# Cross-attention with layer norm on one core: projecting the first query group by column halves, and scoring its first two tiles eight heads at a time

## The chip, the core and the metric

The kernel runs on one of the cores of a Trainium2 chip. A core has five engines that run their own instruction streams in order: TensorE (PE: matrix products; its weight loads are shown apart as PEld), VectorE (DVE), ScalarE (ACT), GpSimd (POOL) and SyncE (SP), which here only issues transfers. An engine waits where an instruction needs the result of another engine or a transfer. SBUF is the working memory; PE writes to PSUM, which has eight banks of 128 x 512 fp32 numbers.

The metric is the device time of one execution in microseconds. Before the change the median of three runs is 506.8 us (506.09 to 507.09).

## What is computed

```
qs = q @ wq                     # q = x: 4 batches x 2048 rows x 512, fp32
ks_, vs = k @ wk, v @ wv        # k = v = ctx: 4 x 77 x 512
scores = einsum('bhqd,bhkd->bhqk', qs, ks_) / sqrt(32)      # 16 heads of 32
attn_w = softmax(where(mask, -inf, scores))
out = einsum('bhqk,bhkd->bhqd', attn_w, vs) @ wo + q
return layernorm(out) * gamma + beta
```

There are 8192 query rows in all, 77 keys to a batch, sixteen heads, and a mask of rows by keys. Everything is fp32. The kernel gets near fp32 accuracy from TensorE's faster float32r format: each operand is split into a high part and the rest, and a product is three matmuls (high x high, high x rest, rest x high).

## The kernel before, in words

Rows are taken in 64 tiles of 128, and the queries are projected in groups of 512 rows, four tiles to a group. The queries of a group are four blocks `m` of 128 columns, that is, of four heads; a block takes twelve matmuls (four contraction steps `c` of three products) into one PSUM bank and is then copied to SBUF (`q_visit`, `q_evac`).

For a tile the stages are these. `scores` (L308): 32 products of 32 contraction rows and 64 query rows, which PE runs side by side, for all sixteen heads, into four banks; bank `j` holds the heads `4g + j`. `maxima` (L357, DVE, one instruction to a head): adds the mask bias, takes the row maximum, and writes the biased scores to SBUF. `exps` (L375, ACT, one to a head): the exponential, with its row sum. `recip` (L383, DVE) and `normalise` (L387, POOL): division by the sum. `transp` (L405, DVE) and `regroup` (transfers issued by SP): weights with keys on the partitions. Then, on pairs of tiles, `av` (L452, PE: weights times values), its split by ACT and DVE, `o_proj` (L546, PE), the residual, the layer norm and the store.

Nothing reorders the program: an engine does its instructions in the order in which the Python code emits them, so a call's place in the code is its place in five queues. From tile 6 on, the order comes from the strings `PAIR` and `ORDER`. The first tiles are done by a prologue written out line by line (L683 to L755) and by a loop over `u = 0, 2, 4` (L769), which handles the tiles `u` and `u + 1`. The table `early` (L759) says which query blocks are projected in which step.

The prologue in order:
- Eight warm-up matmuls and eighteen short ones (L691 to L694).
- Loads: the first 256 rows of group 0's x (transposed, from the array `xT0`) and the four row blocks of wq (L702), the context and wk, the mask, then the second 256 rows of x (L711).
- Queries of the first 256 rows: for each `c` the splits of x and wq, then twelve matmuls of 256 columns, three products for each of the four `m` (L715 to L731). The four banks are copied out at L735.
- Keys: 48 matmuls of 312 columns (L739), with the splits of the context and of wk ahead of them (L732).
- Splits of the second 256 rows of x (L742), `deal_last` (three copies on ACT that lay the last batch's context beside the others), then `q_visit(0, 0)`: 24 matmuls of 256 columns, which give blocks 0 and 1 of the second 256 rows in one bank (L204).
- The loads of wv (from two queues, behind a `gate` on POOL), the copies of the keys (`keys_evac`: per call one block by ACT and one by DVE), and the loads of x for groups 1 and 2 (L751 to L755). Group 1's x goes into the buffer in which wq was staged.

Step `u = 0` of the loop then has: scores and maxima of tile 0, around the copy of `q_visit(0, 0)`; the casts of group 1's x on ACT and the exponentials of tile 0; `q_visit(0, 2)` (blocks 2 and 3 of the second 256 rows); the loads of wo; scores and maxima of tile 1; the differences of wv (`split_wv`); the exponentials of tile 1; and on PE group 1's blocks 0 and 1. Tiles 0 and 1 use rows 0 to 255 of group 0, tiles 2 and 3 the others.

A transfer is issued when its queue comes to it; SP's queue also waits where a buffer is still being read.

## Time and profile before

| | |
|---|---|
| median of three runs | 506.8 us |
| the profiled execution | 508.02 us, of which its span 506.2 us |
| granted TensorE clock | 0.997 of full speed |
| PE idle from 5.07 to 40.65 us | 0.00 us |
| PE idle from 40.65 to 53.45 us | 0.00 us |
| PE idle from 53.45 to 76.85 us | 1.48 us |

The span reaches from the first to the last instruction of the profiled execution; what is beyond it, 1.8 us, lies around it. In the page and the views, a line of a timeline gives start and length in us, engine, source line, operation, the tile written and the tiles read, their shapes, and in brackets the idle time ahead with what ended it. A line of the chain of waits gives start, length, engine, tile and line. A line of the stretches gives the busy time and count of PE, PEld, DVE, ACT and POOL, then the granted clock, the share of the transfer engines, and GB/s. Matmuls overlap, and the ends of their records are modelled.

### The profile page before, as it was taken

Reading aid. Unit: us, or ns where it says so; the run is one execution under the profiler, and the core shown is the slowest. Engines: PE = TensorE matmul, PEld = TensorE weight load, DVE = VectorE, ACT = ScalarE, POOL = GpSimd, SP = SyncE. Lnnn points to the kernel's source line nnn. Section 1 sums busy time; section 2 is a strip of 40 time slices with the busy share of each in tenths; the row PEclk is TensorE's granted clock in tenths of the full one; section 3 lists DMA queues with packets and bytes.
Section 4 is the critical chain, followed back from the end, with each engine's and each line's share of the span. In section 5 each row is a group of like instructions: output and inputs, shape, how many; then the busy total and the mean of one; then the engine's idle time right before and its main releaser. Section 6 shows DMA issues by size and latency. Waiting matters only on the chain.

```text
span 506.2 us, 20441 instructions
## 1 busy us (share of the span) xinstructions
PE 497.0 (98%) x6908; PEld 391.7 (77%) x6908; DVE 463.0 (91%) x2567; ACT 473.0 (93%) x2240; POOL 427.6 (84%) x384
## 2 busy tenths in 40 slices
PE   9999999999999999999999999999999999999995
PEld 7987678777777877777787777778777777777784
DVE  6698899999989988999998998999999889999997
ACT  6798899999999999999999999999999999999971
POOL 0559367989988988989998888999988888999995
PEclk9999999999999999999999999999999999999998
DMA  8945867677887778878777877877778787677665
GB/s 314 388 168 149 222 187 194 190 196 202 231 229 218 223 201 219 229 209 229 213 219 211 232 199 223 229 224 227 216 196 221 199 247 235 170 189 222 167 210 208
DMA packets 58280, 109.50 MB, mean 216 GB/s; under 512 B 9203, under 2 KB 10739, under 8 KB 58176
## 3 DMA queue, kind: packets, MB, share of 16 engines
q1 hardware_dynamic: 55776, 103.35, 71.7%
q0 software_dynamic: 1872, 4.20, 2.8%
q8 instruction: 55, 0.90, 0.8%
q10 hardware_dynamic: 528, 0.66, 0.4%
q14 instruction: 49, 0.40, 0.3%
HBM read 41.68 MB, written 16.78 MB: 115 GB/s over the span
## 4 chain that ended last, share of the span: by engine, by line
PE 79%; DVE 8%; ACT 7%; DMA 2%; issue 1%; SPq 1%; POOL 0%; POOLq 0%; DVEq 0%; ACTq 0%
PE pq L192 27%; PE po L564 26%; PE pa L459 10%; ACT pbuf L379 7%; PE sc L321 6%; DVE B L413 2%; PE sc L564 2%; DVE pbuf L364 2%; PE sc_e L321 2%; PE pk L218 1%; PE pq L725 1%; PE pq L190 1%; PE sc_f L321 1%; SPq L425 1%; DMA out<-o 1%
## 5 line engine op out<-in xcount | busy, mean ns | idle before, releaser
L379 ACT ACTIVATE pbuf<-pbuf,nm 128x77 f32<-128x77 f32 x1024 | 352.6, 349 | 8.6 <-DVE nm L364 7.8
L379 ACT ACTIVATION_READ_ACCUMULATOR pbuf<-pbuf,nm 128x1 f32 x1024 | 193.9, 189 | 0.0
L390 POOL TENSOR_TENSOR pbuf<-pbuf,ri 128x1232 f32<-128x1232 f32 x63 | 145.9, 2316 | 20.8 <-DVE ri L385 17.4
L364 DVE CUSTOM_DVE_ANT_0 pbuf<-sc,mb 128x77 f32<-128x77 f32 x828 | 143.9, 231 | 6.9 <-PE sc L321 6.4
L192 PE MATMUL pq<-xtl,wqh 128*128 128x512 f32 (+1 forms) x256 | 98.3, 384 | 0.0
L192 PE MATMUL pq<-xth,wql 128*128 128x512 f32 (+1 forms) x256 | 98.2, 384 | 0.0
L413 DVE STREAM_TRANSPOSE B<-pbuf 128x1280 f32<-128x1280 f32 x63 | 94.6, 1503 | 0.4
L564 PE MATMUL po<-woh,AH 128*128 128x512 f32 x224 | 90.7, 405 | 0.0
L192 PE MATMUL pq<-xth,wqh 128*128 128x512 f32 (+1 forms) x230 | 88.6, 385 | 0.0
L564 PE MATMUL po<-wol,AH 128*128 128x512 f32 x224 | 87.3, 390 | 0.0
L592 POOL TENSOR_TENSOR o<-o,gam 128x512 f32<-128x512 f32 x53 | 68.7, 1295 | 21.5 <-ACT o L588 21.5
L564 PE MATMUL po<-woh,AL 128*128 128x512 f32 x224 | 86.5, 391 | 0.0
L364 DVE DVE_READ_ACCUMULATOR2_ANT nm<- 128x1 f32 x1024 | 84.4, 82 | 0.0
L593 POOL TENSOR_TENSOR o<-o,bet 128x512 f32<-128x512 f32 x53 | 68.3, 1289 | 4.2
L180 POOL TENSOR_TENSOR xtl<-xtf,xth 128x1024 fp32r<-128x1024 f32 x28 | 67.4, 2409 | 0.1
L459 PE MATMUL pa<-PT,vsb 96*32 96x256 f32 x960 | 58.2, 382 | 1.6 <-DVE vsb L267 1.0
L321 PE MATMUL sc<-kct,q 32*64 32x77 f32 x3312 | 56.0, 238 | 0.5 <-DVE q L209 0.5
L192 PEld LDWEIGHTS pq<-xth,wql 128*128 128x128 f32 x256 | 48.2, 188 | 8.4
L192 PEld LDWEIGHTS pq<-xtl,wqh 128*128 128x128 f32 x256 | 48.1, 188 | 8.4
L321 PEld LDWEIGHTS sc<-kct,q 32*64 32x64 f32 x3312 | 49.3, 130 | 6.5 <-issue 4.4
L564 PEld LDWEIGHTS po<-woh,AH 128*128 128x128 f32 x224 | 42.0, 188 | 10.7 <-DVE nm L364 0.4
L192 PEld LDWEIGHTS pq<-xth,wqh 128*128 128x128 f32 x230 | 43.2, 188 | 9.0
(191 smaller groups left out, 855.1 us busy)
## 6 DMA issues: line engine op xcount, KB each, us to landing
PT<-B SPq DMA_DIRECT2D x355, 128.0 KB
xtf<-xT SPq DMA_DIRECT2D x28, 512.0 KB
o<-x SPq DMA_DIRECT2D x56, 256.0 KB
out<-o SPq DMA_DIRECT2D x56, 256.0 KB
PT<-B POOLq DMA_DIRECT2D x16, 128.0 KB, 4.5
o_end<-x SPq DMA_DIRECT2D x7, 256.0 KB
out<-o_end SPq DMA_DIRECT2D x7, 256.0 KB
xtf<-xT SPq DMA_DIRECT2D x4, 256.0 KB
```

The costliest lines, as they stand in the source:

```text
L180: nc.gpsimd.tensor_tensor(l, fx.pop((g, c)), h.bitcast(F32), ALU.subtract)
L190: nc.tensor.matmul(pq[:, cols], wc, r[:, c, cols], start=False, stop=False)
L192: nc.tensor.matmul(pq, wc, r[:, c, rs], start=(n == 0), stop=(n == 11))
L321: nc.tensor.matmul(scs[t][g, j][r0 : r0 + n], qd[t // 4][q, g, at : at + n], kct[q, g, t // TPB, keys_of(j)], start=True, stop=True,)
L364: nc.vector.tensor_tensor_reduce(pb[:, i // 2, (i % 2) * NK : (i % 2 + 1) * NK], scs[t][g, j], mb[:, t % TPB, keys_of(h)], -1.0, CEIL, ALU ...
L379: nc.scalar.activation(p, p, AF.Exp, bias=nmax[t][:, i : i + 1], scale=-1.0, accum_out=sums[t][:, i : i + 1])
L390: nc.gpsimd.tensor_tensor(pv, pv, rv.to_broadcast((P, NP, 2, NK)), ALU.mult)
L413: nc.vector.transpose(bt.rearrange("p c q r -> p q c r"), pbuf[t % NPB].rearrange("p q (c r) -> p q c r", c=5),)
L459: nc.tensor.matmul(pas[b, g // 2][HD * j : HD * (j + 1), (g % 2) * BLK : (g % 2 + 1) * BLK], vsb[:, 2 * b // TPB, HD * h : HD * (h + 1)], ...
L564: nc.tensor.matmul(pos[t], a[:, c, rs], w[:, c], start=(first and n == 0), stop=(n == 11))
L592: nc.gpsimd.tensor_tensor(o, o, gam, ALU.mult)
L593: nc.gpsimd.tensor_tensor(o, o, bet, ALU.add)
```

## The change

Group 0 is projected with all its 512 rows in each matmul, but in two column halves. The first half (blocks 0 and 1, heads 0 to 7) stands where the first 256 rows stood, ahead of the keys: 24 matmuls of 512 columns. So wq is now stored and loaded by column halves, the first half with x at the start and the second where the second 256 rows of x were loaded; x is loaded whole, one contraction step to a transfer. The second half of wq is split behind wk.

Behind the keys come at once the scores of heads 0 to 7 of tiles 0 and 1 (`scores_first((0, 1))`), with their maxima; then the other two query blocks, and then the scores of heads 8 to 15 of both tiles. Block 3 is copied out by ACT (rows 0 to 255) and DVE (rows 256 to 511), each half of the bank (`q_evac_both`). The exponentials of heads 0 to 7, the casts of group 1's x and ACT's half of that copy share ACT in a written-out order. `deal_last` moves between the two calls of `keys_evac`, the first two differences of wv go ahead of the copy of block 3 and the other two behind the second maxima, and the loads of wo, the identity and the first `recip` and `normalise` follow them. In step `u = 2` the first two differences of wo move on POOL from ahead of group 2's x differences to behind them. Step `u = 0` is no longer in the loop.

```diff
     def q_evac(g, m):
+        nc.vector.tensor_copy(qd[g][:, m, :], qp.pop((g, m)))
+
+    def q_evac_both(g, m):
         pq = qp.pop((g, m))
-        if g: ...
+        for cols, copy in zip(HALVES, (nc.scalar.copy, nc.vector.tensor_copy)):
+            copy(qd[g][:, m, cols], pq[:, cols])
...
+    def scores_first(gs):
+        own = [bank(f"sc_0_{gs[0]}_{j}") for j in range(GH)]
+        units = [(t, g) for g in gs for t in (0, 1)]
...
+        for t, g in units:
             for half in range(0, P, P // 2):
                 for j in range(GH):
                     score(t, g, j, half, P // 2)
...
-    for c in range(0, NC_D, 2):
-        nc.sync.dma_start(f0[c][:, 0], xT0[0, :, c : c + 2])
-        (nc.sync if c else nc.scalar).dma_start(stage_a[:, 0, c], wview(wq, c))
-        nc.sync.dma_start(stage_a[:, 0, c + 1], wview(wq, c + 1))
+    wqf = stage_a[:, 0].rearrange("p c e -> p (c e)").rearrange("p (a c e) -> p a c e", a=2, c=NC_D)
+    for c in range(NC_D):
+        nc.sync.dma_start(fx[0, c // 2 * 2][:, c % 2], xT[0, :, c])
+        if c < 2:
+            nc.scalar.dma_start(wqf[:, 0, c], wq[:, 0, c])
+        elif c == 2:
+            nc.sync.dma_start(wqf[:, 0, 2:], wq[:, 0, 2:])
...
     load_mask(0)
     for c in range(0, NC_D, 2):
-        nc.sync.dma_start(f0[c][:, 1], xT0[1, :, c : c + 2])
+        nc.sync.dma_start(wqf[:, 1, c : c + 2], wq[:, 1, c : c + 2])
...
-        for n, (w, r) in enumerate(((wqh, x0h), (wqh, x0l), (wql, x0h))):
-            for m in range(NG):
+        prods = ((wqh, x0h), (wqh, x0l), (wql, x0h)) if c else ((wqh, x0h), (wql, x0h), (wqh, x0l))
+        for n, (w, r) in enumerate(prods):
+            for m in range(2):
                 nc.tensor.matmul(
-                    pq0[m][:, :BLK],
+                    pq0[m],
...
+    for c in range(NC_D):
+        split_wq(1, c)
+    nc.scalar.copy(qd[0][:, 0], pq0[0])
+    nc.vector.tensor_copy(qd[0][:, 1], pq0[1])
...
-    deal_last()
-    q_visit(0, 0)
     mask_bias(0, slice(0, TPB // 2))
     gate(stage_a[:, 1, NC_D - 1, D - 1 :])
     load_wv()
-    for m in range(0, NG, 2):
-        keys_evac(pks, m)
+    keys_evac(pks, 0)
+    deal_last()
+    keys_evac(pks, 2)
...
+    heads_a, heads_b = ([GH * g + j for j in range(GH) for g in gs] for gs in ((0, 1), (2, 3)))
+    scores_first((0, 1))
+    maxima_of(0, heads_a)
+    maxima_of(1, heads_a)
+    q_visit(0, 2)
+    q_visit(0, 3)
+    q_evac(0, 2)
+    exps_of(0, heads_a[:3])
+    cast_xT(1, 0)
+    split_xT(1, 0)
+    exps_of(0, heads_a[3:7])
+    cast_xT(1, 2)
+    split_xT(1, 2)
+    exps_of(0, heads_a[7:])
+    exps_of(1, heads_a[:2])
+    mask_bias(0, slice(TPB // 2, TPB))
+    split_wv((0, 1))
+    q_evac_both(0, 3)
+    exps_of(1, heads_a[2:])
+    scores_first((2, 3))
+    maxima_of(0, heads_b)
+    maxima_of(1, heads_b)
+    exps_of(0, heads_b)
+    split_wv((2, 3))
+    load_wo()
...
+    recip(0)
+    normalise(0)
+    exps_of(1, heads_b)
+    evac = visits(1)
+    for q in evac:
+        q_visit(*q)
+    for u in range(2, JOIN, 2):
```

`maxima_of` and `exps_of` are `maxima` and `exps` with a list of heads; `split_wq(a, c)` makes the high part and the rest of half `a`, step `c`, of wq, the high parts on ACT but for the very first, which DVE makes.

## The prediction

> **What bounds the kernel now.** I began with the page's busy times, because they say which engine can't be made later without making the end later.

> ```profile
> span 506.2 us, 20441 instructions
> ...
> PE 497.0 (98%) x6908; PEld 391.7 (77%) x6908; DVE 463.0 (91%) x2567; ACT 473.0 (93%) x2240; POOL 427.6 (84%) x384
> ```

> PE is idle for only 506.2 - 497.0 = 9.2 us. The busy times by stretch say where; the columns are PE, PEld, DVE, ACT, POOL, then clock and DMA.

> ```profile
> 5.07:40.65 35.58, 35.58 (x396) 32.10 (x397) 29.22 (x136) 30.53 (x124) 17.98 (x15) 1.00 0.78 281
> ...
> 53.45:76.85 23.40, 21.92 (x355) 16.11 (x353) 20.81 (x119) 21.38 (x111) 10.92 (x9) 1.00 0.75 199
> 106.20:450.00 343.80, 343.72 (x4937) 269.06 (x4930) 321.38 (x1869) 338.41 (x1632) 312.31 (x259) 1.00 0.78 215
> ```

> From its first real matmul at 5.07 to 40.65 PE never stops. In the middle 344 us it stops for 0.08 us, and ACT is close behind (338.41 of 343.80). So whatever the start gains or loses on PE reaches the end unchanged, unless the ramp between 53.45 and 76.85, where PE idles 1.48 us, swallows or returns it. The third view is the chain of waits, where the change lies: start, length, what.

> ```profile
> 0.73 3.54 DMA xtf<-xT
> 4.29 0.72 ACT xth L154 x2
> 5.07 5.98 PE pq L725 x48
> 11.05 7.03 PE pk L218 x48
> 18.08 2.87 PE pq L192 x24
> 20.95 0.88 PE sc L321 x55
> 21.83 3.06 PE pq L192 x24
> 24.89 0.88 PE sc L321 x55
> 25.77 5.67 PE pq L192 x24
> 31.44 0.88 PE sc L321 x54
> 32.32 2.96 PE pv L258 x12
> 35.28 5.44 PE pq L192 x24
> 40.72 0.89 PE sc L321 x54
> 41.93 4.97 ACT pbuf L379 x29
> 47.73 1.45 DVE B L413
> ```

> It is PE's program order from 5.07 to 41.6: first half of group 0's queries, keys, second half in two visits with the scores of tiles 0 and 1 between them, group 1's queries, scores of tile 2, values, group 1 again, scores of tile 3. Only then do exponentials (ACT) and transposes (DVE) carry the chain. The two waits that matter to ACT are these.

> ```profile
> 33.27 1.98 ACT L176 CAST xth<-xtf 128x1024 fp32r<-128x1024 f32 x2
> ...
> 41.93 0.36 ACT L379 ACTIVATE pbuf<-pbuf,nm 128x77 f32<-128x77 f32 x1 [1.18 <-DVE nm L364]
> ```

> ACT is done with the exponentials of tiles 0 and 1 at 33.27, and later waits 1.18 us for tile 3's maxima, which wait for the scores that PE reaches at 40.65. ACT's earlier work is thus not on the path: only the moment at which PE reaches tile 3's scores counts. The question is how much the change moves that moment.

> **Part 1: fewer, wider query matmuls.** Before, group 0 takes 96 matmuls of 256 columns: 5.98 + 2.87 + 3.06 = 11.91 us of the chain. After, it takes 48 of 512 columns. A 512-wide run of 24 costs 5.44 behind other matmuls (35.28) and 5.67 behind a score visit (25.77). The first of the two runs begins the chain: a 256-wide run of 48 costs 2 x 2.87 = 5.74 in the stream and 5.98 at the start, so a start adds 0.24; 5.44 + 0.24 = 5.68. The second run comes behind scores: 5.67. Together 11.35, a gain of 0.56 us on PE.

> [...]

> **Part 2: the start.** Each of the four contraction steps still needs 384 KB (128 of x and 256 of wq before, 256 and 128 after), and the splits on ACT and DVE have the same total width.

> ```profile
> 4.32 0.69 PE L694 MATMUL pw<-ident 128*128 128x32 bf16 x18
> ...
> 5.02 0.62 ACT L154 CAST wqh<-stage_a 128x512 fp32r<-128x512 f32 x1
> ...
> 7.13 0.62 ACT L154 CAST wqh<-stage_a 128x512 fp32r<-128x512 f32 x1 [1.05 <-DMA stage_a<-wq]
> ```

> The warm-up matmuls end at 5.01, so PE can't begin earlier by more than 0.06. The first x cast is now 512 wide (0.62) and, from the same landing at 4.27, ends at 4.91: PE still begins at about 5.07. The third weight block landed at 7.13; PE needs its counterpart at 5.07 + 5.68 / 2 = 7.9, behind a 256-wide cast. I take 0 for the start, with bounds of -0.06 and +0.5 (two steps that wait 0.25 each, half of that DMA wait in all). The changed order of the first three products and ACT's second DMA issue are covered by the same wait for the first landing; uncovered, each would delay PE by its own length.

> **Part 3: from the keys to the first scores.** PE leaves the keys at 5.07 + 5.68 + 7.03 = 17.78 (18.08 before, so 0.30 earlier). Before, 2.87 us of queries covered the copying of the keys; now eight-head scores come directly behind them.

> ```profile
> 14.59 0.52 ACT L251 CAST ctx_h<-ctx_h 128x384 fp32r<-128x384 f32 x1
> 15.01 0.36 ACT L251 CAST ctx_lAH<-ctx_lAH 128x192 fp32r<-128x192 f32 x1
> 15.26 0.36 ACT L251 CAST ctx_lAL<-ctx_lAL 128x192 fp32r<-128x192 f32 x1
> 16.80 0.55 ACT L232 ACTIVATE kct<-pk 128x308 f32<-128x308 f32 x2 [1.18 <-PE pk L218]
> ...
> 17.24 0.62 DVE L234 TENSOR_SCALAR kct<-pk 128x308 f32<-128x308 f32 x2 [0.92 <-PE pk L218]
> ```

> The first visit needs only key blocks 0 and 1, whose copies end 0.30 earlier than these, at 17.05 (ACT) and 17.56 (DVE): before 17.78, so no wait. If this cover of 0.22 us fails, PE waits by the difference. ACT then deals the last batch's context columns (15.62 - 14.59 = 1.03) and copies block 2 (0.55), until 18.63, which nobody needs before the second visit. The scores take 0.88: the first visit ends at 18.66, 3.2 us earlier than tile 0's sixteen heads did (21.83); now it is eight heads of two tiles.

> **Part 4: the wait that is added.** Behind that visit PE runs 5.67 us of queries, to 24.33, and next come the second eight heads of both tiles. They need the fourth query block, whose last matmul has only just gone by. Before, each score visit used queries that had been copied out long ago. So PE stands still for one copy.

> ```profile
> L736 ACT COPY q<-pq x2: 362/368/374, 13.0 to 13.3; 128x256 f32<-128x256 f32 x2
> ...
> L737 DVE COPY q<-pq x2: 412/414/416, 13.9 to 14.2; 128x256 f32<-128x256 f32 x2
> ...
> 31.05 0.39 PE L192 MATMUL pq<-xth,wql 128*128 128x512 f32 x1
> 31.37 0.95 PE L321 MATMUL sc<-kct,q 32*64 32x77 f32 x64
> ```

> Tiles 0 and 1 read rows 0 to 255, the half that ACT copies in 0.37. A handoff costs about 0.06 (in the chain the x cast ends at 4.29 + 0.72 = 5.01 and PE starts at 5.07); I take one on each side, though no row shows them here. 24.33 is the last matmul's end, as 31.05 + 0.39 = 31.44 is in these rows. So the visit begins at 24.33 + 0.06 + 0.37 + 0.06 = 24.82 and, no longer overlapped with the matmul ahead (the row says 0.95 against 0.88), ends at 25.77. Before it ended at 25.77, too. The wait has eaten what the wider matmuls brought. Bounds of the wait: 0.36 (the copy alone) and 0.96 (both halves in turn, 0.37 + 0.41, with three handoffs). Queued behind PE's wait are all of group 1's queries.

> ACT must be free by 24.39. The exponentials run at this pace, and ahead of the copy stand ten of them and two casts.

> ```profile
> L379 ACT ACTIVATE pbuf<-pbuf,nm 128x77 f32<-128x77 f32 x32 | 11.0, 350 | 0.0
> ...
> 19.36 1.05 ACT L176 CAST xth<-stage_a 128x1024 fp32r<-128x1024 f32 x1 [1.12 <-DMA stage_a<-xT]
> 21.33 1.05 ACT L176 CAST xth<-stage_a 128x1024 fp32r<-128x1024 f32 x1 [0.93 <-DMA stage_a<-xT]
> 22.29 0.36 ACT L379 ACTIVATE pbuf<-pbuf,nm 128x77 f32<-128x77 f32 x1
> ```

> Thirty-two lie between 22.29 and 33.27: 0.343 each. The first can start some 0.3 behind the visit (41.93 against 40.72 + 0.89), at 19.0; a cast in a row of two takes 0.99 (33.27). Three end at 20.0; cast to 21.0; four to 22.4; cast to 23.4; three to 24.4: just in time. It needs the two x transfers at 20.0 and 22.4, against 19.36 and 21.33 in the trace: 0.6 and 1.1 us to spare. DVE has sixteen maxima, a copy, a mask piece and two of wv's differences before its half; PE does not wait for that half.

> **Part 5: what moves behind cover.** The second column half of wq is split where the second half of x was, in the same 2 us before the keys end. The halves of wv's differences move to both sides of the second visit; values need them at 32.32, some 3 us later. Uncovered, values would start late by what is missing there. wo's loads, the identity and wo's differences are not used before the transposes of tile 2 (47.73); the first two normalisations come earlier on POOL than before. Uncovered, they would push those transposes, one for one. ACT ends tiles 0 and 1 at 19.0 + 32 x 0.343 + 1.98 + 0.37 = 32.3 rather than 33.27, and then waits about 0.9 us longer for tile 3.

> **Sum.** -0.56 + 0.49 (the wait) + 0.07 (0.95 - 0.88) = **0.0 us** at 25.77, carried to the end. The profiled execution took 508.02 us for a span of 506.2; it would become 508.0 and 506.2. The unprofiled median, 506.8 of runs between 506.09 and 507.09, becomes **506.8**; about 0.2% (1.0 us) is what a measurement can tell from no change.

> **Rivals.** *Slower: the late x transfer.* The second piece of group 1's x goes into the buffer where the second half of wq now lies, so SP can issue it only when DVE has split that half: at about 15.3, when the next load went out that waited for such a split, and no longer by 13.12.

> ```profile
> 12.32 0.80 SPq L753 DMA_DIRECT2D stage_a<-xT  x2
> 15.27 0.93 SPq L171 DMA_DIRECT2D xtf<-xT  x2
> ```

> If it lands later by the same 2.5 us, at 23.8 instead of 21.33, the cast ends at 24.8, three exponentials at 25.8, the copy at 26.2, and the second visit begins at 26.3, 1.4 us later: 508.2. It decides from a landing after 22.4. For it: ACT is strictly in order and waited 0.93 for this transfer. Against: it took over 8 us from issue to landing, so it stood in a queue, and the queue's order is unchanged. *Waiting for both halves.* Both copies read one bank; if the scores wait for DVE's half too, 0.45 more: 507.2. *Faster: ACT's lead counts.* ACT is 98% busy in the middle stretch. If ACT is what the later stretches wait for, its lead of 33.27 - 32.3 = 0.9 us reaches the end: 505.9, and 505.8 with the wait's low bound. Against it stands the wait of 1.18 at 41.93, which would simply grow. [...]

> **How the numbers follow.** Forecast 0.59, both halves 0.10 (also within 0.2%), late transfer 0.13, ACT's lead 0.18. The lead lies on the bound of 0.2%; I count two thirds of it as faster. So faster is 0.12, no change 0.59 + 0.10 + 0.06 = 0.75, slower 0.13. The forecast's own range is 505.9 to 507.6: the bounds of start and wait (-0.2 and +0.5) and the runs' spread (-0.7 and +0.3). For the lead I reach down to 505.3, half the spread below its 505.8, and for both halves, with their spread, up to 507.9; what is left out is the late transfer and a little of the lead.

> **What would show it.** Right: 24 matmuls of 512 columns from 5.07, first exponential near 19.0, PE idle some 0.5 us before the second visit at about 24.8, tile 2's scores within 0.2 us of 31.4 and tile 3's of 40.7, and ACT's wait at 41.9 grown to about 2 us. Wrong: tile 3's scores moved by over 0.5 us, or the same start and yet another time at 76.85.

## The result, and the profile after

The kernel after the change took 511.27 us (median of 8 runs, 508.69 to 513.77) against 506.88 us before (8 runs, 506.09 to 508.78): a ratio of 1.0081, 95% interval 1.0053 to 1.0109. Measured again beside later experiments it took 509.49 us (12 runs, 508.57 to 514.02) against 506.90: 1.0063, interval 1.0041 to 1.0085. So the change makes the kernel slower by 2.6 to 4.4 us, where the forecast was no change.

The page of the profiled execution (512.25 us) begins:

```profile
span 510.1 us, 20346 instructions
...
PE 499.6 (98%) x6860; PEld 390.2 (76%) x6860; DVE 467.2 (92%) x2568; ACT 474.2 (93%) x2242; POOL 428.1 (84%) x384
```

There are 48 matmuls fewer, as planned, and yet PE is busy for 2.6 us longer. The chain of waits shows where the start goes (start, length, what):

```profile
0.73 3.57 DMA stage_a<-wq
...
4.32 6.99 DMA stage_a<-wk
...
11.32 0.63 ACT woh L153
...
11.98 0.70 DVE wol L154
...
12.73 7.03 PE pk L214 x46
19.76 0.88 PE sc L332 x52
20.64 5.67 PE pq L191 x24
26.31 0.45 PE sc L332 x32
...
26.77 0.53 PE sc L332 x32
27.30 5.67 PE pq L191 x24
...
42.25 0.88 PE sc L332 x52
...
55.38 1.86 PE pa L476 x32
```

Before, the start of the chain was PE's own work from 5.07 on. Now a transfer of wk carries it: it is issued at 4.32 and ends 7 us later, and only then can that part of wk be split. Two of the 48 key matmuls run ahead of it; the other 46, which the chain shows, run from 12.73 on, where before all 48 ran from 11.05 on. PE leaves the keys at 19.76 instead of 18.08, 1.68 us later, and tile 3's scores are 1.53 us late (42.25 against 40.72). The stretches show the transfers at that time; the last three columns are the clock, the share of the transfer engines and GB/s. First before, then after:

```profile
5.00:6.00 1.00, 0.94 (x9) 0.96 (x9) 1.00 (x3) 0.95 (x2) 0.00 (x0) 1.00 1.04 326
6.00:7.00 1.00, 1.00 (x11) 1.00 (x10) 1.00 (x3) 0.08 (x1) 0.00 (x0) 1.00 1.04 393
```

```profile
5.00:6.00 1.00, 1.00 (x4) 0.81 (x4) 0.68 (x2) 0.63 (x2) 0.00 (x0) 1.00 0.75 158
6.00:7.00 1.00, 1.00 (x6) 0.82 (x5) 0.97 (x2) 0.40 (x2) 0.00 (x0) 1.00 0.77 246
```

Where 326 and 393 GB/s were moved, there are now 158 and 246. In after's ACT timeline the splits wait for it, above all for wq's last piece:

```profile
5.37 0.62 ACT L153 CAST xth<-xtf 128x512 fp32r<-128x512 f32 x1 [0.58 <-DMA xtf<-xT]
...
6.89 0.62 ACT L153 CAST xth<-xtf 128x512 fp32r<-128x512 f32 x1 [0.60 <-DMA xtf<-xT]
...
8.70 0.40 ACT L724 CAST wqh<-stage_a 128x256 fp32r<-128x256 f32 x1 [1.18 <-DMA stage_a<-wq]
```

PE, which before never stopped here, stands still until that split is done:

```profile
9.15 0.73 PE L752 MATMUL pq<-xth,wqh 128*128 128x512 f32 x2 [0.76 <-ACT wqh L724]
```

The second loss is far away. PE's timeline near 429 us, with the idle time and its releaser in brackets: first one row of before (its second profile, `before2` below), where the 64 products of this visit run through in 0.95 us, then after, then after's stretches around it:

```profile
427.04 0.95 PE L321 MATMUL sc<-kct,q 32*64 32x77 f32 x64
```

```profile
428.68 0.94 PE L332 MATMUL sc<-kct,q 32*64 32x77 f32 x62
431.22 0.29 PE L332 MATMUL sc<-kct,q 32*64 32x77 f32 x2 [1.60 <-issue]
```

```profile
432.00:434.00 2.00, 2.00 (x7) 1.55 (x6) 2.00 (x11) 2.00 (x13) 1.95 (x3) 0.67 0.35 87
434.00:436.00 2.00, 2.00 (x6) 1.54 (x5) 2.00 (x19) 2.00 (x13) 2.00 (x3) 0.50 0.30 69
436.00:438.00 2.00, 2.00 (x10) 1.64 (x10) 1.97 (x5) 2.00 (x14) 1.85 (x2) 0.98 0.84 233
```

In the middle of a score visit, two products before its end, PE stands still for 1.60 us and waits for nothing that the profile shows. Then the granted clock falls to 0.67 and 0.50, which loses 0.66 + 1.00 us more. This is most of why PE's busy time grew: the same matmuls at a lower clock. The page of the profile names one more thing that could run dry there, TensorE's program itself, which arrives by a queue of its own:

```profile
q8 instruction: 54, 0.88, 0.8%
```

That is 0.88 MB in 54 packets, 16 KB each, for 2 x 6860 = 13,720 matmuls and weight loads: an estimate from these is 64 bytes to an instruction (0.88 MB / 13,720) and about 254 instructions to a packet (13,720 / 54), which the experiments below take as 256. In the stretch from 428 to 429 us the view of the transfers shows one of these packets (0.02 MB). That the queue is TensorE's shows in before and `g1_period` (fourth batch), which differ in the warm-up alone: the second has 256 instructions of TensorE more, and one packet more.

```profile
q8 instruction: 55, 0.90, 0.8%
```

```profile
q8 instruction: 56, 0.92, 0.9%
```

### The profile page after: what moved, and what is told of

Same layout as the page of the kernel before. It is cut to its first block, busy times and chain, and to the rows that moved or that the text cites. A ratio compares the mean times of both kernels' runs of the same rounds, so it can differ in the third digit from the quotient of the medians.

```text
span 510.1 us, 20346 instructions
## 1 busy us (share of the span) xinstructions
PE 499.6 (98%) x6860; PEld 390.2 (76%) x6860; DVE 467.2 (92%) x2568; ACT 474.2 (93%) x2242; POOL 428.1 (84%) x384
## 4 chain that ended last, share of the span: by engine, by line
PE 86%; ACT 4%; DVE 4%; DMA 3%; issue 1%; POOL 0%; SPq 0%; POOLq 0%; ACTq 0%
PE pq L191 30%; PE po L581 28%; PE pa L476 11%; PE sc L332 7%; ACT pbuf L396 3%; PE sc L581 2%; PE sc_e L332 2%; PE pv L254 2%; DMA PT<-B 1%; PE pk L214 1%; DMA stage_a<-wk 1%; PE pq L189 1%; PE sc_f L332 1%; DMA stage_a<-wq 1%; DVE pbuf L378 1%
## 5 line engine op out<-in xcount | busy, mean ns | idle before, releaser
L191 PE MATMUL pq<-xth,wql 128*128 128x512 f32 x248 | 97.6, 393 | 0.0
L191 PE MATMUL pq<-xtl,wqh 128*128 128x512 f32 x248 | 97.4, 393 | 0.0
L191 PE MATMUL pq<-xth,wqh 128*128 128x512 f32 x222 | 87.8, 396 | 0.0
L191 PEld LDWEIGHTS pq<-xtl,wqh 128*128 128x128 f32 x248 | 47.0, 189 | 8.9
L191 PEld LDWEIGHTS pq<-xth,wql 128*128 128x128 f32 x248 | 47.0, 189 | 8.9
L191 PEld LDWEIGHTS pq<-xth,wqh 128*128 128x128 f32 x222 | 42.1, 190 | 9.5
```

What stands on the lines that cost most here:

```text
L191: nc.tensor.matmul(pq, wc, r[:, c, rs], start=(n == 0), stop=(n == 11))
```

## The experiments

**First batch: start, place in the program, or chance.** `a1_pad` adds 48 warm-up matmuls (96 instructions with their weight loads), so that behind the warm-up TensorE's program stands where it stood in before.

```diff
-WARM = 8
+WARM = 3
-    for i in range(18):
+    for i in range(71):
```

> The changed kernel with 3 long and 71 short warm-up matmuls instead of 8 and 18: 48 more PE matmuls, so that from group 1 on PE's instructions stand at the same places of its 256-instruction blocks as in the kernel before; the short ones take about as long as the long ones left out, and PE waits for its loads there anyway. Theory A (PE's program is fetched in blocks, and a shift by 96 instructions puts a block's end ahead of dense score visits, where PE runs dry and the clock then drops): no stall of over 1 us in the middle, about 507.2 us (before plus the 0.4 us by which the ramp's end was late). Theory B (the late loads of the start are what is paid): no change, about 511. Theory C (such stalls come by chance in any program): a spread as wide as that of the changed kernel, about 511.

`b1_shift` does the reverse to the kernel before: 80 matmuls (160 instructions) more, which is 96 fewer modulo 256.

```diff
-WARM = 8
+WARM = 1
-    for i in range(18):
+    for i in range(105):
```

> The kernel before with 1 long and 105 short warm-up matmuls instead of 8 and 18: 160 PE instructions more, which is the changed kernel's shift of -96 but for one block of 256; nothing else changes. Theory A: a stall of 1 to 2 us in the middle in some or all runs, 508 to 511 us. Theory B: as before, 506.9 (plus up to 0.3 if the warm-up ends later). Theory C: as before, 506.9.

`a2_layout` is after with other host arrays: each piece of group 0's x and of wq is contiguous. In after the pieces are rows of 1 or 2 KB that lie 8 KB apart from partition to partition.

```diff
-        nc.sync.dma_start(fx[0, c // 2 * 2][:, c % 2], xT[0, :, c])
+        nc.sync.dma_start(fx[0, c // 2 * 2][:, c % 2], xT0[c])
...
-            nc.scalar.dma_start(wqf[:, 0, c], wq[:, 0, c])
+            nc.scalar.dma_start(wqf[:, 0, c], wqa[c])
...
-            nc.sync.dma_start(wqf[:, 0, 2:], wq[:, 0, 2:])
+            nc.sync.dma_start(wqf[:, 0, 2:], wqb[0])
```

> The changed kernel with group 0's x and wq stored so that each of the first transfers reads one contiguous piece of memory; the transfers and their order stay. If the 2 KB pieces that lie 8 KB apart are what slows the start: over 350 GB/s between 5 and 7 us (158 and 246 in the changed kernel), and the keys begin about 1.5 us earlier, near 11.2 us. Theory B: then about 507 us. Theory A: the stall stays somewhere in the middle, 509 to 511 us, since the ramp had already swallowed all but 0.4 us of the late start.

`a3_both` is `a2_layout` with the warm-up of `a1_pad`.

> Both: contiguous first transfers and 48 more warm-up matmuls. PE's first real matmul waits for the warm-up here if that takes longer than the loads. Theory A: no stall in the middle, 506.9 to 507.3 us. Theory B: 507 as well. Theory C: 509 or more with a wide spread.

Medians beside 506.89 for before: `a1_pad` 509.23 (1.0040, interval 1.0027 to 1.0053), `b1_shift` 509.03 (1.0041, 1.0029 to 1.0053), `a2_layout` 507.97 (1.0023, 1.0014 to 1.0032), `a3_both` 507.02 (1.0015, 0.9997 to 1.0033). The layout takes most of the loss back, and layout and warm-up together all that can be measured. With the layout mended the loads move 358 and 407 GB/s from 5 to 7 us and the keys begin at 11.50, about as expected if the scattered rows slow the start. Theory A had `a1_pad` at 507.2 and theory B at 511, and for `a2_layout` it was 509 to 511 against 507; both came out between the two. So neither the start nor the place in the program carries the loss alone. Most telling is PE's timeline of `b1_shift`, a kernel that has nothing of the change but a shifted program:

```profile
427.70 0.92 PE L321 MATMUL sc<-kct,q 32*64 32x77 f32 x61
429.15 0.35 PE L321 MATMUL sc<-kct,q 32*64 32x77 f32 x3 [0.52 <-issue]
```

It stops in the same visit as after. `a2_layout`, also shifted, has 0.69 us there, while `a1_pad` and `a3_both` have no such stop. `a1_pad` proves less than was hoped: its warm-up ended at 4.29, PE then stood still for 0.97 us, and up to 8.8 us its pairs of query matmuls took 1.03 us or more, where later pairs take 0.62. PE also had a gap of 0.89 us at 494 us. Slow first pairs show in `a2_layout` too (1.21 and 1.05 us, then 0.62), so what its start still loses need not come of the loads.

**Second batch: which array, which wait, which profile.** `c1_x` is after with x alone contiguous, `c2_wq` with wq's pieces alone.

> The kernel after, with group 0's x stored contiguously for each contraction step (in after each partition's 2 KB lie 8 KB apart); wq stays as in after. After's keys start at 12.73 us, with both x and wq contiguous at 11.50, before at 11.05. Theory X (the scattered x is what slows the loads): keys start near 11.5 and the loads move about 400 GB/s from 5 to 7 us. Theory Q (the scattered halves of wq, pieces of 1 and 2 KB, slow them): keys still start near 12.7, and the rate still falls below 250 GB/s between 5 and 7 us. Theory XQ (each carries part, by bytes in pieces of 2 KB): near 12.1.

> The kernel after, with the pieces of wq's column halves stored contiguously; x stays as in after. Theory X: keys still start near 12.7. Theory Q: near 11.5, at about 400 GB/s from 5 to 7 us. Theory XQ: near 12.1.

None of the three theories held. The chains, first of `c1_x`, then of `c2_wq`:

```profile
11.29 7.04 PE pk L215 x48
```

```profile
11.43 7.05 PE pk L215 x48
```

Either array alone brings the keys from 12.73 back to about 11.4, and between 5 and 7 us the loads move 386 and 380 GB/s (`c1_x`), 326 and 356 (`c2_wq`). So it is not one slow array: only x and wq together, both as rows 8 KB apart, bring the rate of these two microseconds down to 158 and 246. Scattered x alone costs less: in `c2_wq` PE waits 0.65 us for x's first cast and begins at 5.66. Why the two together lose so much stays open.

`c3_order` is after with the second visit of scores in the other order.

```diff
-        for t, g in units:
+        for t, g in units[2:] + units[:2] if gs[0] else units:
```

> The kernel after, with the second visit of scores in the other order: first the 32 products that read the query block 3, which has only just been copied, then the 32 that read block 2. In after the visit ends 0.99 us behind the last matmul ahead of it, 0.11 more than the 0.88 of a visit that waits for nothing, where the prediction had 1.44. Theory W: the copy does take the predicted 0.49 us, but the visit begins with 32 products that need block 2 only, and they fill the wait; then it is uncovered here, the visit ends about 1.4 us behind the matmul, and tile 2's scores come 0.4 later from the keys' start than in after (20.6 instead of 20.2 us). Rival: the wait itself is as short as 0.11 us; then the visit stays at 0.99.

PE's timeline of `c3_order`:

```profile
25.39 0.39 PE L191 MATMUL pq<-xth,wql 128*128 128x512 f32 x1
26.24 1.13 PE L332 MATMUL sc<-kct,q 32*64 32x77 f32 x64 [0.46 <-ACT q L207]
```

Now the wait stands open: 0.46 us, for ACT's copy, and the visit ends at 27.37, 1.59 us behind the last matmul (25.78) instead of 0.99. Theory W is right in kind: the wait was there and had been covered. The visit ends 0.2 us later than the expected 1.4, since its products take 1.13 us instead of 0.95, and why they do stays open.

`before2` is the kernel before, profiled once more.

> The kernel before, profiled a second time. Its first profiled execution took 508.02 us against a median of 506.88 and had a gap of 1.00 us on TensorE ahead of the first product of weights and values (53.84 to 54.84 us), which no profile of a changed kernel has. If that gap belongs to the one execution: no gap here, that product begins near 53.9 us, and the span is near 505.1. If it belongs to the kernel: the gap is here again, and the start's delay in after was partly swallowed by it.

Its chain, and the stretch of the ramp:

```profile
10.94 7.03 PE pk L218 x48
...
53.73 1.86 PE pa L459 x32
```

```profile
53.45:76.85 23.40, 22.89 (x446) 17.02 (x444) 21.68 (x124) 22.36 (x113) 12.15 (x9) 1.00 0.79 207
```

The first profile had this row at the same place:

```profile
54.84 1.93 PE L459 MATMUL pa<-PT,vsb 96*32 96x256 f32 x32 [1.00 <-DVE vsb L267]
```

That gap of 1.00 us belonged to that one execution; none of the fifteen other profiles has it. In this one (506.64 us, span 504.8) PE idles in the ramp for 23.40 - 22.89 = 0.51 us, not 1.48, and the chain is PE's own up to the scores that begin at 55.59. Against 53.73, the step that begins at 55.38 in after is 1.65 us late: the start's loss is carried in full. With it the first profile of after is accounted for, but for 0.4 us: its span is 5.3 us longer than this one (510.1 against 504.8), and start, stop and low clock make 1.65 + 1.60 + 1.66 = 4.91.

**Third batch: the stall again, and the outside.** `after2` is the kernel after, and `c1_timed` is `c1_x`, both timed. `e1_xpad` is `c1_x` with 48 more warm-up matmuls, of a length that leaves the start alone.

```diff
-WARM = 8
+WARM = 5
-    for i in range(18):
+    for i in range(69):
```

> The kernel after, timed again beside the others of this batch. Theory S (TensorE's program arrives in blocks and a stall in the middle comes of where the blocks fall; with the change 96 instructions fewer lie ahead of the middle): the median is again about 511, since the start costs 1.7 us and the outside of the span 0.3, which gives 508.9, and stalls bring some 2 more; its profile has a stall of TensorE near 429 us. Theory C (the stalls come by chance, and the first measurement had many): about 509, with single runs above, and in any kernel alike.

> The kernel after with x alone contiguous, timed. In its one profile the keys began at 11.29 us and weights times values at 53.95, 0.2 later than in the kernel before. Start and outside (0.2 + 0.3) give 507.4. Theory S: some 0.5 to 2 more, 507.9 to 509.4, as the place in TensorE's program is that of after. Theory C: 507.4, with single runs above.

> The one before, with 5 long and 69 short warm-up matmuls instead of 8 and 18: TensorE's first real matmul comes at about the same time, and from there on its program stands where it stood in the kernel before. Theory S: 507.2 to 507.5, without a stall near 429 us, so 0.5 to 2 below the one before. Theory C: the same as the one before, within 0.3.

`c1_timed` took 508.51 (1.0030, interval 1.0013 to 1.0046), `e1_xpad` 506.77 (0.9996, 0.9981 to 1.0011). These two have the same instructions but for the warm-up, and their products of weights and values begin at 53.97 and 53.73; yet they are 1.74 us apart. PE's timeline of `c1_timed`:

```profile
428.92 0.29 PE L333 MATMUL sc<-kct,q 32*64 32x77 f32 x2 [0.76 <-issue]
```

In `e1_xpad` that visit runs through. `after2`'s profile stops there as well, for 0.50 us, without a fall of the clock. Its median of 509.49 is nearer to theory C's 509 than to theory S's 511; it is the stop in its profile, and the pair of `c1_timed` and `e1_xpad`, that speak for S. `e1_xpad` came out lower than S had it (507.2 to 507.5).

`d1_oneact` is `a3_both` with one transfer of the start on ACT instead of two.

```diff
-            nc.scalar.dma_start(wqf[:, 0, c], wqa[c])
+            (nc.sync if c else nc.scalar).dma_start(wqf[:, 0, c], wqa[c])
```

> The kernel with contiguous x and wq and the warm-up of 3 and 71 (median 507.02), with the second piece of wq issued by SP instead of ACT, so that ACT issues one transfer, as in the kernel before. All kernels with the change have 2.1 us of their time outside the span, the kernel before and its shifted variant 1.8. If ACT's second transfer is the cause: 1.8 outside, and a median of about 506.7. If not: 2.1 outside and 507.0, or later if SP's issue of one more transfer holds up x.

It took 506.58 (0.9995, interval 0.9976 to 1.0013). Time less span lies between 1.77 and 1.87 us in its twelve runs, as in all runs of before (1.73 to 1.85 in that batch); in those of `after2`, `c1_timed` and `e1_xpad` it lies between 2.07 and 2.19. So ACT's second transfer at the start costs 0.3 us outside the span; why it does stays open.

**Fourth batch: a whole block, and all repairs.** `g1_period` is before with 128 more warm-up matmuls (`WARM = 1` and 153 short ones); `f1_best` is `e1_xpad` with one transfer on ACT.

> The kernel before with 128 more warm-up matmuls (1 long and 153 short instead of 8 and 18), so that 256 more instructions of TensorE lie ahead of the first real one: one whole block of 16 KB, if an instruction is 64 bytes. The variant with 160 more (80 matmuls) stalled 0.52 us at 428.62 and took 509.03. The warm-up ends later, so the start is some 1 us late; read the delay from where weights times values begin (53.73 in the second profile of before). Theory S (the place within the block counts): no stall near 428, and time less delay is 506.9, within 0.4. Rival L (a longer warm-up, whatever its length, brings the stall): a stall of 0.5 near 429, and time less delay near 508.5.

> The kernel after with all three repairs: x contiguous, one transfer on ACT, the warm-up of 5 and 69. The version with x and warm-up alone had 506.77, the version with one transfer (and another warm-up) 1.83 outside the span instead of 2.12. If the three add up: 506.5, which is 0.4 below the kernel before at 506.9, inside the 0.2% that can be told apart. If SP's additional issue delays x at the start: 506.8.

`g1_period` took 507.71 (1.0016, interval 1.0006 to 1.0027). Its chain:

```profile
54.84 1.86 PE pa L459 x32
```

That is 1.11 us late: the long warm-up ends at 5.56 only, and the keys then wait for the split of wk. 507.71 - 1.11 = 506.6: a whole block more costs nothing in the middle, and PE does not stop near 429 us, while `b1_shift`, with a shorter warm-up, did. Rival L falls. `f1_best` took 507.15 (1.0013, interval 0.9996 to 1.0030) with a start 0.55 late in its profile; 506.5 to 506.8 was expected. It does not beat before: like `a3_both`, `e1_xpad` and `d1_oneact` it is level with it.

The table puts the timed runs together. "Stall" and "start" come from one profile of each kernel, and the two profiles of after differ by 0.55 us in the start, so the last column is good to about half a microsecond. "Start" is the beginning of weights times values less 53.73; "outside" is 0.3 with two transfers on ACT; "rest" is what is left of the difference to before.

| kernel | instructions ahead | stall near 429 | difference | start | outside | rest |
|---|---|---|---|---|---|---|
| after | -96 | 1.60 | +4.39 | 1.65 | 0.3 | 2.4 |
| `after2` | -96 | 0.50 | +2.59 | 1.10 | 0.3 | 1.2 |
| `c1_timed` | -96 | 0.76 | +1.61 | 0.24 | 0.3 | 1.1 |
| `a2_layout` | -96 | 0.69 | +1.08 | 0.46 | 0.3 | 0.3 |
| `b1_shift` | +160 | 0.52 | +2.14 | 0.51 | 0 | 1.6 |
| `a1_pad` | 0 | none | +2.34 | 1.61 | 0.3 | 0.4 |
| `a3_both` | 0 | none | +0.13 | -0.57 | 0.3 | 0.4 |
| `e1_xpad` | 0 | none | -0.13 | 0.00 | 0.3 | -0.4 |
| `d1_oneact` | 0 | none | -0.32 | -0.18 | 0 | -0.1 |
| `f1_best` | 0 | none | +0.28 | 0.55 | 0 | -0.3 |
| `g1_period` | +256 | none | +0.84 | 1.11 | 0 | -0.3 |

The rest is 1.3 us on average in the five shifted kernels and 0.0 in the six others; single values meet (`a2_layout` has 0.3, `a1_pad` and `a3_both` 0.4). Theory S (theory A of the first batch) holds in the counts that were tried: what counts is how many instructions of TensorE stand ahead, and 256 more are as good as none. It holds in every profile. The visit near 429 us takes 0.95 us in all eight profiles of programs that are not shifted (both of before among them). Of the eight of shifted ones, six stop there, `c3_order` with 0.49 us among them, and in `c1_x` and `c2_wq`, which show no idle time, the visit takes longer:

```profile
427.22 1.19 PE L333 MATMUL sc<-kct,q 32*64 32x77 f32 x64
```

```profile
427.19 1.25 PE L333 MATMUL sc<-kct,q 32*64 32x77 f32 x64
```

There, too, the last two products are late: they begin 0.90 and 0.96 us behind the visit's first, against 0.71 in `e1_xpad`. That PE waits for its program is not named by the profile, which only says "issue", but the packets bear it out. In the traces of the eight shifted programs the last packet ahead of these products lands between 0.60 us before the visit's beginning (`c1_x`) and 0.93 us after it (after). The later it lands, the later, by and large, come the last products, from 0.90 to 2.54 us behind the visit's beginning; in all eight that is 1.24 to 1.61 us after the landing. So the size of the stall goes with the arrival of a packet. That the shift decides whether PE needs it in the middle of a visit is argued from this, and what makes up the 1.24 to 1.61 us stays open. The size of a packet agrees with what the shifts did: 0.88 MB in 54 packets makes about 254 instructions to each, and a shift by 256 leaves no stall (`g1_period`, 506.6 us without its late start), while one by 160 brings one (`b1_shift`, 0.52 us).

## Why the prediction was wrong, point by point

**Part 2, the start, is the step that failed.** "Each of the four contraction steps still needs 384 KB", so "I take 0 for the start, with bounds of -0.06 and +0.5". The bytes are indeed the same, but they were costed at the old rate. The diff showed that x now comes as `xT[0, :, c]` and wq by column halves, both in rows 8 KB apart; nothing in the prediction asked what that does to the rate. In after the rate between 5 and 7 us fell to 158 and 246 GB/s from 326 and 393, and PE waited 0.76 us for wq's last piece and then for wk. That put the products of weights and values back by 1.65 and 1.10 us in the two profiles of after, outside the bounds. Undoing the scatter of either array takes nearly all of it back (0.22 us is left in `c1_x`, 0.37 in `c2_wq`).

**What lay around the span was held constant**: "508.0 and 506.2". ACT's second transfer was named, and costed only as covered by the wait for the first landing; it adds 0.3 us outside the span (`d1_oneact`, `f1_best`).

**The middle was held constant too.** No term or rival had the length of the program in it. A change that only removes matmuls was credited with their time and with nothing else; it also moved all that follows by 96 instructions. That is the term which was missing altogether; it is what the table's rest of 2.4 and 1.2 us in the two measurements of after is put down to.

**Part 4, the wait, was over-costed.** The copy behaves as predicted: in after's ACT timeline ACT comes just in time.

```profile
24.27 1.03 ACT L175 CAST xth<-stage_a 128x1024 fp32r<-128x1024 f32 x1
...
26.34 0.37 ACT L207 COPY q<-pq 128x256 f32<-128x256 f32 x1
```

But the prediction had PE stand still for 0.49 us. In the chain above PE begins the visit at once: 32 products (0.45 us) read block 2, which DVE had copied from 23.62 on, and at 26.77 the other 32 start. The visit ends 0.99 us behind the matmul, 0.11 more than one without a wait and not the predicted 0.56. `c3_order` shows the whole wait when that cover is taken away.

**Parts 1 and 3 were right in kind.** The second run of 24 takes the predicted 5.67. The first takes 5.77 where loads hardly disturb it (`c2_wq`; 5.68 predicted). The first visit follows the keys without a wait. From the keys' end to group 1's first matmul it is 27.30 - 19.76 = 7.54 us, against 25.66 - 17.97 = 7.69 in `before2`; the prediction had 25.77 - 17.78 = 7.99. PE's own path thus gained a little, as the sum without the wait said, and the start and the middle ate it.

**"Whatever the start gains or loses on PE reaches the end" was right, and the exception was not.** Of the 1.48 us in the ramp that might have swallowed it, 1.00 came of one untypical execution.

**The rivals.** The late x transfer did not come: the cast at 24.27 shows no wait. Waiting for both halves did not come either: DVE copies its half at 29.20 in after, when PE has long left the visit (27.30). ACT's lead did not come: its wait for tile 3's maxima is 0.69 us in after, less than the 1.18 before, and not the predicted 2. The time fell on the slower side, by mechanisms that were not among them.

## What to carry to other kernels

When a load keeps its bytes but changes its rows, cost it anew, and with it the loads that run beside it: two scattered arrays together lost far more than either alone (the keys began at 12.73 us with both, at 11.29 and 11.43 with one, at 11.05 before). Where PE never waits, a change that adds or removes its instructions should be timed with the program padded back to its old place as well, or a shift of blocks is taken for the change (`c1_timed` and `e1_xpad`, which differ in the warm-up alone, are 1.74 us apart). Before a gap is called slack, look whether a second profile has it; and before a wait is added to a sum, look which of the waiting instructions really need what is late.

## What the runs showed of the hardware

One gap of 1.60 us was followed by reduced clock (0.67, then 0.50, then 0.98 in stretches of 2 us); gaps of 0.49 to 0.76 us in the other shifted kernels were not (1.00 from 428 to 438 us in `b1_shift` and `c1_timed`, 1.00 from 76.85 to 450 us in `after2`, a mean of 0.999 over all of `a2_layout` and `c3_order`).

A second transfer on ACT's queue at the start lengthens the time outside the span from 1.8 to 2.1 us: it is 1.73 to 1.89 us in every timed run with one and 2.07 to 2.19 us in every timed run with two.
